# Two matmul groups of a block's preparation moved into the two-bank place of the attention scores, parts of the keys moved to GpSimd, and the first maxima taken over two banks

## The chip, the core and the metric

The kernel runs on one core of one Trainium2 chip. The metric is the device time of a whole launch in microseconds (us), the median of several runs. Engines are named as the profile names them: PE (TensorE, matmuls), PEld (its weight loads), DVE (VectorE), ACT (ScalarE), POOL (GpSimd) and SP (SyncE, which here issues nearly all DMAs).

## The reference, cut to what matters

```
# x: (1, 4096, 256); 16 heads of 16; r = 32
proj = quant4(x) @ ternary_weight(Wqkv).T + b      # one projection for Q, K and V
q = proj.reshape(B, N, h, dk).transpose(0, 2, 1, 3)
k = v = proj.reshape(B, h, N, dk)                  # a head's keys: 256 rows of proj
q, k = rotary(q), rotary(k)
att = (q @ U) @ (k @ U).T / sqrt(dk)               # i.e. q (U U^T) k^T
y = softmax(att) @ v
x = layernorm(x + quant4(y) @ ternary_weight(Wo).T)
x = layernorm(x + ffn(x))                          # 256 -> 1024 -> 1024 -> 1024 -> 256
```

`quant4` scales each row by its largest magnitude and rounds it to whole numbers from -8 to 7. `ternary_weight` gives signs, with zeros below a threshold, times a row's mean magnitude.

## The kernel before, in words

The work is cut into 8 blocks of 512 rows and 8 pairs of heads. A *unit* is one pair of heads against one block of queries, so there are 64; the first eight units are pair 0 with blocks 0 to 7. A unit has 32 *steps*. In a step s PE does three things for different units:

- `largest(s)`: two matmuls (L632), one for each head of the pair, make 128x512 scores each in a bank of PSUM from the pool `ps_1` (three banks), and two DVE reductions (L640) take their row maxima. This is a first pass that finds the largest score of each query.
- `weights(s - 40)`: 40 steps later (`LAG`), four matmuls (L678) make the scores less the maxima in a place of two banks, called `sc` (pool `ps_sc`, two such places, used in turn), and one ACT exponential of 128x1024 (L686) writes them to SBUF as `pr`.
- `values`: every second step, eight matmuls (L700) multiply two steps' `pr` with V into `av`.

So for the first 40 steps there is only the first pass (the *ramp*), and then both passes run side by side. A new unit's maxima have to go through DRAM to become rows (`largest_parts` L652 and L653, `largest_rows` L659 to L667) before its `weights` can start.

The order on all engines is written out by hand. `at(step, f)` puts a piece of work into a list, and the loop at the end calls, for each step, what is listed for it and then `largest` and `weights`. A step is thus only a place in each engine's order. An engine does its own list as soon as its data are there; GpSimd and SP can be far ahead of or behind PE's step.

Within the ramp and pair 0, the seven later blocks are also prepared, each during one unit. For block b, with `first = 32(b-1)`:

- the block of x is loaded 24 steps ahead, its row maxima are taken on DVE (`biggest`, L129, four times), and POOL makes the whole numbers (`integers`, L148 to L152);
- at first+5, `tables`: the rows' scale goes through DRAM and comes back spread over all partitions (L445, L447), and the cosines are loaded (L337);
- at first+7, `transposed`: eight PE transposes (L158) and an ACT copy (L160);
- at first+9 and first+11, `even_odd`: the projection of the even and of the odd columns, two matmuls each (L459), into one bank of `ps_1` each; ACT scales (L467), POOL multiplies by the scale and adds the bias (L468, L469) into `eo`;
- at first+12, `queries`: POOL rotates and splits them into a high and a low part (L484 to L492); SP stores them in DRAM (L497, first+23), and loads them as `qT` of the next unit (L590, at step 25 of the unit before), so that `largest` of block b can start at step 32b;
- at first+13 and first+15, `natural`: the block's V (`project`, L170), in one bank of `ps_1` each, with ACT (L603) and later POOL (L606, L607);
- at first+16, `rotate_keys` on POOL (L510 to L513), at first+29 `regroup_keys` by DMA (L521), at first+34 and first+36 `times_g`: the keys times U U^T (L529, one matmul instruction of two passes each), into one bank of `ps_1` each; ACT copies the high part (L531), DVE makes the low part (L532); SP stores them (L570) for the later pairs.

Block 0 is prepared ahead of the ramp by `set_up`, which also prepares the signs of both weight matrices. Its keys are spread over partitions by `place_keys` (L558), in places of `sc`, one group for each of the first eight steps.

After pair 0 there are seven pairs with no block to prepare, and then the feed-forward part.

Of the kernel before, what the change touches and what calls it, by code (L numbers as in the profile page):

```python
# [9 lines left out]
F32 = mybir.dt.float32  # L10
# [8 lines left out]
P = 128  # L19
# [18 lines left out]
def attn_ffn_kernel(  # L38
# [53 lines left out]
    sgn_o = const.tile([P, 2, D], BF16, name="sgn_o")  # L92
    alpha_o = const.tile([P, D], F32, name="alpha_o")
    bias_bc = const.tile([P, D], F32, name="bias_bc")
    scales = {}
# [203 lines left out]
    with ExitStack() as actx:  # L299
# [31 lines left out]
        def bank1(shape, dt):  # L331
            return ps_1.tile(shape, dt, name="ps1")
# [7 lines left out]
        def set_up():  # L340

            nc.sync.dma_start(out=x_bufs[0], in_=x_t[:, ts(0, BT), :])
            tw = [ppool.tile([P, 2, D], F32, name=f"tw{i}", tag="pr") for i in range(2)]
            wabs = ppool.tile([P, 2, 2, D], F32, name="tabs", tag="pr")
            neg = ppool.tile([P, 2, 2, D], F32, name="tneg", tag="pr")
            nc.sync.dma_start(out=tw[0], in_=wqkvT.rearrange("(k p) o -> p k o", p=P))
            set_picks()
# [12 lines left out]
            nc.sync.dma_start(out=cs_k, in_=csk)  # L360
            ps = magnitudes(tw[0], wabs[:, 0], bank1)
            biggest(None)
# [3 lines left out]
            nc.sync.dma_start(out=x_bufs[1], in_=x_t[:, ts(1, BT), :])  # L366
            nc.sync.dma_start(out=tw[1], in_=woT.rearrange("(k p) o -> p k o", p=P))
            nc.sync.dma_start(out=bias_bc, in_=bqkv.partition_broadcast(P))

            set_constants()  # L370
            for e in range(2):
                for k in range(2):
                    nc.tensor.matmul(
                        ps[:, D + e : D + e + 1],
                        lhsT=wabs[:, 0, k, e::2],
                        rhs=ones[:, :1],
                        start=(k == 0),
                        stop=(k == 1),
                    )
# [10 lines left out]
            transposed()  # L390
            signs(tw[0], neg[:, 0], ps, sgn_qkv, alpha_qkv)
            nc.vector.tensor_scalar(alpha2, ps[:, D : D + 2], 1.0 / D, None, ALU.mult)
            nc.vector.tensor_tensor(gmat, psg[:, :P], mask, ALU.mult)

            def output_weights():
                ps = magnitudes(tw[1], wabs[:, 1], bank1)
                return lambda: signs(tw[1], neg[:, 1], ps, sgn_o, alpha_o)

            return held, output_weights

# [51 lines left out]
        def even_odd(b, held, o):  # L452
# [17 lines left out]
            else:  # L470
# [3 lines left out]
                nc.scalar.activation(x, x, AF.Identity, bias=bias2_sb[:, o : o + 1])  # L474

        def two(key):
            return [rot.tile([P, 2, QB], F32, name=f"{key}{i}") for i in range(2)]
# [48 lines left out]
        def times_g(b, held, x):  # L526
# [5 lines left out]
            nc.vector.tensor_tensor(low, ps, high.bitcast(F32), ALU.subtract)  # L532

        def place_queries(held, qT):

            ps = bank1([P, QB], F32)
            for n in range(4):
                h, i = divmod(n, 2)
                nc.tensor.matmul(
                    ps,  # L540
                    lhsT=pick_q[:, h, i],
                    rhs=held["parts"][:, h, i],
                    start=(n == 0),
                    stop=(n == 3),
                )
            nc.scalar.copy(qT, ps)

        def place_keys(held, kT, g, banks={}):

            if g % 2 == 0:  # L550
                banks[0] = ps_sc.tile([P, 2, QB], F32, name="sc")
            ps = banks[0][:, g % 2]
            for k in range(2):
                x, c = divmod(2 * g + k, 8)
                for n in range(4):
                    j, i = divmod(n, 2)
                    o = 80 - 64 * j - DK * i
                    nc.tensor.matmul(  # L558
                        ps[:, ts(k, N // H)],
                        lhsT=pick_k[:, c, o : o + P],  # L560
                        rhs=held["parts"][:, 2 + x, i, ts(j, N // H)],
                        start=(n == 0),
                        stop=(n == 3),
                    )
            nc.scalar.copy(kT[:, ts(g, QB)], ps)
# [28 lines left out]

        def natural(b, held, i0):

# [13 lines left out]

            project(held, sgn_qkv, bank1, i0, evacuate)

# [4 lines left out]
        yas, yts, y4s, ys = {}, {}, {}, {}  # L617
        todo = {}

        def at(step, f):  # L620
            todo.setdefault(step, []).append(f)

        def largest(s):

            u, i = divmod(s, NKT)
            qt, ck = divmod(i, NKT // BT)
            if i == 0:
                mxs[u] = stat.tile([P, BT, 2, NKT // BT], F32, name="mx")
            ps = [ps_1.tile([P, 512], F32, name="ps1") for j in range(2)]
            for j in range(2):  # L630
# [7 lines left out]
                )  # L638
            for j in range(2):
                nc.vector.tensor_reduce(  # L640
                    mxs[u][:, qt, j, ck : ck + 1], ps[j], AX.X, ALU.max
                )
            if i == NKT - 1:
# [173 lines left out]
        with tc.manual_schedule():  # L817
# [5 lines left out]
            at(NKT * (NQB + 2 * len(chunks)), set_flag)  # L823
            first_held, output_weights = set_up()
            even_odd(0, first_held, 0)
            even_odd(0, first_held, 1)
            output_signs = output_weights()
            rotate_keys(0, first_held, nc.vector)
# [3 lines left out]
            qTs[0] = qpool.tile([P, QB], F32R, name="qT", bufs=3)  # L832
            times_g(0, first_held, 0)
            place_queries(first_held, qTs[0])
            place_keys(first_held, kTs[0], 0)
            output_signs()
            times_g(0, first_held, 1)
            for g in range(1, 8):
                at(g - 1, lambda g=g: place_keys(first_held, kTs[0], g))
            at(2, lambda: store_queries(0, first_held))  # L840
            for i in range(2):
                at(4 + i, lambda i=i: natural(0, first_held, 2 * i))
            at(6, lambda: [f() for f in first_held["rest"]])
            for b in range(1, NQB):
                first = NKT * (b - 1)
                h, biggest, measure, integers, transposed = quantize_steps(
                    x_bufs[b % 2], bank1, nc.gpsimd, ma_parts[b % 2][:, :BT]
                )
                if b > 1:
                    at(  # L850
                        first - 24,
                        lambda b=b: nc.sync.dma_start(out=x_bufs[b % 2], in_=x_t[:, ts(b, BT), :]),
                    )
                    for i in range(BT):
                        at(first - 15 + 2 * i, lambda i=i, f=biggest: f(i))
                    for i, f in enumerate(measure):
                        at(first - 7 + 2 * i, f)
                else:
                    biggest(None)
                    for f in measure:  # L860
                        f()

                def tables(b=b, h=h):
                    start_scales(b, h)
                    h["cs"] = load_tables(b)

                at(first - 1 if b > 1 else 0, integers)
                at(first + 5, tables)
                at(first + 7, transposed)
                for o in range(2):  # L870
                    at(first + 9 + 2 * o, lambda b=b, h=h, o=o: even_odd(b, h, o))
                at(first + 12, lambda b=b, h=h: queries(b, h))
                at(first + 23, lambda b=b, h=h: store_queries(b, h))
                for i in range(2):
                    at(first + 13 + 2 * i, lambda b=b, h=h, i=i: natural(b, h, 2 * i))
                at(first + 16, lambda b=b, h=h: rotate_keys(b, h, nc.gpsimd))
                at(first + 17, lambda h=h: [f() for f in h["rest"]])
                at(first + 29, lambda h=h: regroup_keys(h))
                for x in range(2):
                    at(first + 34 + 2 * x, lambda b=b, h=h, x=x: times_g(b, h, x))  # L880
                    at(first + 37, lambda b=b, h=h, x=x: store_keys(b, h, x))

# [5 lines left out]
            for u in range(NU):  # L888
# [12 lines left out]
                if u:  # L901
                    at(NKT * (u - 1) + (25 if u < NQB else 14), lambda u=u: load_queries(u))
                base = NKT * u + LAG
# [48 lines left out]
            for s in range(NKT * NU + LAG + AVLAG + 4):  # L952
                while todo.get(s):
                    todo[s].pop(0)()

# [217 lines left out]
```

## Time and profile before

| | |
|---|---|
| median of 3 runs | 3589.16 us (3588.69 to 3589.31) |
| the profiled execution | 3586.87 us |
| its span in the profile | 3585.0 us |
| PE busy | 3544.8 us (99%) |
| DVE busy | 3044.8 us (85%) |
| ACT busy | 2337.1 us (65%) |
| POOL busy | 432.2 us (12%) |
| first exponential (the ramp's end) | 91.01 us |
| last exponential | 2907.13 us |

Busy time is counted from the start of an instruction to its modelled end, so a PE that is shown 100% busy can still lose time between matmuls. The time from one `values` group to the next (a *pair of steps*) is the better ruler: in most of the kernel it is 2.70 us.

### The profile page before, as it was taken

The numbers are of one execution on the slowest core, as the hardware profiler recorded it, in microseconds if no ns is written. First come the engines' busy times: TensorE is split into PE (matmuls) and PEld (weight loads), VectorE is DVE, ScalarE is ACT, GpSimd is POOL, SyncE is SP. The second block draws the span as 40 slices with busy tenths as digits, with TensorE's granted clock in tenths as the row PEclk, the third lists the DMA queues.
The fourth block names the chain that finished last, engine by engine and source line by source line (L and its number), as shares of the span: only waits on it lengthen the run. The fifth ranks groups of instructions, "written<-read, shape, count | busy, mean of one in ns | idle before, by whom it ended". The sixth has DMA issues, their size and how long they took to land.

```text
span 3585.0 us, 61100 instructions
## 1 busy us (share of the span) xinstructions
PE 3544.8 (99%) x23824; PEld 1996.1 (56%) x23831; DVE 3044.8 (85%) x5612; ACT 2337.1 (65%) x2710; POOL 432.2 (12%) x525
## 2 busy tenths in 40 slices
PE   7999999999999999999999999999999999999998
PEld 4444455555555555555555555545555458888887
DVE  8888999999999999999999999999999945555554
ACT  2777777777777777777777777777777753333332
POOL 5766300000000000000000000000000010000000
PEclk7999999999999999999999999999999999999999
DMA  3343212111211121112111111211121130000000
GB/s 92 91 112 100 58 27 50 27 27 27 50 27 29 30 50 27 27 27 51 28 27 43 34 27 27 44 27 23 47 68 33 24 91 1 29 25 18 18 7 13
DMA packets 267634, 141.74 MB, mean 40 GB/s; under 512 B 184520, under 2 KB 243656, under 8 KB 266440
## 3 DMA queue, kind: packets, MB, share of 16 engines
q1 hardware_dynamic: 263512, 126.22, 14.3%
q0 software_dynamic: 3824, 11.54, 1.1%
q8 instruction: 189, 3.10, 0.4%
q14 instruction: 109, 0.89, 0.1%
HBM read 91.44 MB, written 42.07 MB: 37 GB/s over the span
## 4 chain that ended last, share of the span: by engine, by line
PE 93%; POOL 2%; DVE 2%; DMA 2%; ACT 0%; issue 0%; SPq 0%; POOLq 0%; ACTq 0%
PE av L700 27%; PE sc L678 25%; PE ps L632 21%; PE ps_mm L997 18%; DVE mx L640 1%; DMA qT<-q_dram 1%; DMA scale<-ma_dram 0%; PE ps L529 0%; DMA ma_dram<-ma_turned 0%; POOL eo L469 0%; POOL qk L492 0%; POOL eo L468 0%; DMA q_dram<-qk 0%; POOL rot L484 0%; POOL rot L485 0%
## 5 line engine op out<-in xcount | busy, mean ns | idle before, releaser
L640 DVE TENSOR_REDUCE mx<-ps 128x1 f32<-128x512 f32 x4096 | 2550.0, 683 | 147.4 <-PE ps L632 93.1
L686 ACT ACTIVATE pr<-sc 128x1024 f32<-128x1024 f32 x2048 | 1991.6, 1021 | 739.4 <-PE sc L678 737.2
L632 PEld LDWEIGHTS ps<-kT,qT 64*128 64x128 f32 x4096 | 567.3, 184 | 985.2 <-DVE mx L640 852.1
L700 PE MATMUL av<-pr,v_all 128*32 128x512 f32 x8192 | 1091.6, 605 | 0.7
L632 PE MATMUL ps<-kT,qT 64*128 64x512 f32 x4096 | 1064.5, 474 | 10.0 <-DMA qT<-q_dram 4.0
L678 PE MATMUL sc<-m_rows,minus 64*128 64x512 f32 x4096 | 821.6, 394 | 0.4 <-DMA m_rows<-m_dram 0.4
L678 PE MATMUL sc<-qT,kT 64*128 64x512 f32 x4096 | 816.3, 392 | 0.0
L678 PEld LDWEIGHTS sc<-m_rows,minus 64*128 64x128 f32 x4096 | 392.6, 185 | 88.0 <-ACT pr L686 36.1
L678 PEld LDWEIGHTS sc<-qT,kT 64*128 64x128 f32 x4096 | 392.9, 184 | 86.7
L700 PEld LDWEIGHTS av<-pr,v_all 128*32 128x32 f32 x8192 | 161.3, 108 | 256.6 <-issue 254.7
L1027 ACT ACTIVATE gate<-ps_mm,sc_hs 128x512 f32<-128x512 f32 x128 | 88.1, 689 | 288.7 <-PE ps_mm L997 248.6
L281 DVE CAST h<-gate 128x512 fp32r<-128x512 f32 x128 | 54.3, 425 | 223.6 <-ACT gate L1027 223.4
L653 POOL TENSOR_TENSOR m_parts<-m,m_parts 128x8 fp32r<-128x8 f32 x64 | 13.0, 203 | 1798.7 <-ACT m_parts L652 1763.5
L283 DVE TENSOR_TENSOR h<-gate,h 128x512 fp32r<-128x512 f32 x192 | 132.3, 689 | 5.1
L997 PE MATMUL ps_mm<-h,h1a 128*128 128x512 f32 x512 | 128.8, 394 | 0.0
L1019 DVE SCALAR_TENSOR_TENSOR gate<-ps_mm,sc_s,gate 128x512 f32<-128x512 f32 x64 | 48.0, 750 | 94.3 <-ACT gate L1017 74.3
L997 PE MATMUL ps_mm<-h,h2a 128*128 128x512 f32 x512 | 127.2, 390 | 0.0
L997 PE MATMUL ps_mm<-h,h1b 128*128 128x512 f32 x512 | 126.5, 389 | 0.0
L997 PE MATMUL ps_mm<-h,h2b 128*128 128x512 f32 x512 | 126.5, 389 | 0.0
L732 DVE STREAM_TRANSPOSE yt<-ya 128x64 f32<-128x64 f32 x504 | 116.8, 232 | 0.0
L997 PEld LDWEIGHTS ps_mm<-h,h1b 128*128 128x128 f32 x512 | 96.1, 188 | 20.1
L997 PEld LDWEIGHTS ps_mm<-h,h2b 128*128 128x128 f32 x512 | 96.1, 188 | 19.9
(178 smaller groups left out, 1636.8 us busy)
## 6 DMA issues: line engine op xcount, KB each, us to landing
y_raw<-yt SPq DMA_DIRECT2D x256, 64.0 KB
qT<-q_dram SPq DMA_DIRECT2D x252, 64.0 KB
y<-y_raw SPq DMA_DIRECT2D x63, 256.0 KB
kT<-k_dram SPq DMA_DIRECT2D x28, 512.0 KB
xs<-in_x SPq DMA_DIRECT2D x16, 512.0 KB
q_dram<-qk SPq DMA_DIRECT2D x32, 256.0 KB
k_dram<-qk SPq DMA_DIRECT2D x56, 128.0 KB
cs_q<-in_csq SPq DMA_DIRECT2D x8, 512.0 KB
```

What stands on the lines that cost most here:

```text
L281: eng(dst[:, k, 0, :], g)
L283: nc.vector.tensor_tensor(dst[:, k, 1, :], g, dst[:, k, 0, :].bitcast(F32), ALU.subtract)
L632: nc.tensor.matmul(ps[j], lhsT=qTs[u][rows, ts(qt, P)], rhs=kTs[u // NQB][rows, ts(ck, 512)], start=True, stop=True,)
L640: nc.vector.tensor_reduce(mxs[u][:, qt, j, ck : ck + 1], ps[j], AX.X, ALU.max)
L653: nc.gpsimd.tensor_tensor(parts[:, :, 1, :], m, parts[:, :, 0, :].bitcast(F32), ALU.subtract)
L678: nc.tensor.matmul(ps[:, j, :], lhsT=minus[rows, :] if first else kTs[u // NQB][rows, ts(kt, P)], rhs=m_rows[u % 2][rows, :] if first else ...
L686: nc.scalar.activation(pr, ps, AF.Exp)
L700: nc.tensor.matmul(avs[u][strip : strip + 32, :], lhsT=v_all[:, 2 * (2 * pair + j) + a, c * (DK + 1) : c * (DK + 1) + 32], rhs=probs[s + k ...
L732: nc.vector.transpose(yts[u][:, ts(i, 64)], yas[u][:, ts(i, 64)])
L997: nc.tensor.matmul(ps, lhsT=sb[:, ks, ts(o, P)] if split else wo[:, k, :], rhs=src[:, k, i, :], start=(k == 0 and i == 0), stop=(k == n - ...
L1019: nc.vector.scalar_tensor_tensor(g, pb, scales["s2"][:, o : o + 1], gate, ALU.mult, ALU.mult)
L1027: nc.scalar.activation(g, ps, AF.Gelu, scale=scales[sc][:, o : o + 1])
```

## The change

It has five parts.

1. From block 2 on, `both_projections` takes the place of the two `even_odd`, `all_natural` that of the two `natural`, and `both_times_g` that of the two `times_g`. Each makes all its matmuls in one go into one two-bank place of `sc`, the places that otherwise hold the scores of `weights`. ACT empties the projections and the products with one 128x1024 copy each, V with four 128x256 ones as before.
2. `key_parts` splits the keys on GpSimd (a copy and a subtraction of 128x1024), where `times_g` used ACT and DVE. The projections' scale, factor and bias are all applied on GpSimd.
3. The steps of a block's preparation change. `tables` comes 8 steps before the unit for blocks 3 and later, x is loaded 30 steps ahead, and the queries of units 4 to 7 are loaded at step 22 where it was 25. The three groups are put into a second list, `later`, so that they stand behind `values` in their step.
4. In the ramp, `largest` puts its two matmuls into one place of `sc`, and one DVE reduction takes both maxima (128x1024 to 128x2). In unit 0 it goes through the keys chunk by chunk, so that a chunk is needed every fourth step only; `place_keys` moves to every second step and into `ps_1`.
5. The output weights' signs leave `set_up`: their sums are taken in the ramp (step 20) and their signs on GpSimd, later. The second block's maxima are taken before the ramp starts, and its preparation moves by some steps.

The core of the diff:

```diff
+        def both_projections(held):
+            held["eo"] = kprep.tile([P, 2, QB], F32, name="eo", tag="kr")
+            ps = ps_sc.tile([P, 2, QB], F32, name="sc")
+            for o in range(2):
+                for k in range(2):
+                    nc.tensor.matmul(ps[:, o], lhsT=sgn_qkv[:, k, o::2], ...)
+            nc.scalar.copy(held["eo"], ps)
+            nc.gpsimd.tensor_tensor(held["eo"], held["eo"], held["scale"]..., ALU.mult)
+            for o in range(2):
+                x = held["eo"][:, o]
+                nc.gpsimd.tensor_scalar(
+                    x, x, alpha2[:, o : o + 1], bias2_sb[:, o : o + 1], ALU.mult, ALU.add
+                )
...
+        def both_times_g(held):
+            ps = ps_sc.tile([P, 2, QB], F32, name="sc")
+            for x in range(2):
+                nc.tensor.matmul(ps[:, x], lhsT=gmat, rhs=held["keys"][:, x], start=True, stop=True)
+            held["kg"] = kprep.tile([P, 2, QB], F32, name="kg", tag="kr")
+            nc.scalar.copy(held["kg"], ps)
+
+        def key_parts(held):
+            high, low = (held["parts"][:, 2:4, i] for i in range(2))
+            nc.gpsimd.tensor_copy(high, held["kg"])
+            nc.gpsimd.tensor_tensor(low, held["kg"], high.bitcast(F32), ALU.subtract)
...
-        def place_keys(held, kT, g, banks={}):
-            if g % 2 == 0:
-                banks[0] = ps_sc.tile([P, 2, QB], F32, name="sc")
-            ps = banks[0][:, g % 2]
+        def place_keys(held, kT, g):
+            ps = bank1([P, QB], F32)
...
+        def all_natural(b, held):
+            both = ps_sc.tile([P, 2, QB], F32, name="sc")
+            for i in range(2):
+                natural(b, held, 2 * i, lambda shape, dt, i=i: both[:, i])
...
-            qt, ck = divmod(i, NKT // BT)
+            qt, ck = divmod(i, NKT // BT) if u else divmod(i, BT)[::-1]
...
-            ps = [ps_1.tile([P, 512], F32, name="ps1") for j in range(2)]
+            both = ps_sc.tile([P, 2, QB], F32, name="sc") if s < LAG else None
+            ps = [ps_1.tile(...) if both is None else both[:, j] for j in range(2)]
...
+            if both is not None:
+                nc.vector.tensor_reduce(mxs[u][:, qt, :, ck], both, AX.X, ALU.max)
...
-                at(first - 1 if b > 1 else 0, integers)
-                at(first + 5, tables)
-                at(first + 7, transposed)
...
+                    at(first + 2 if b == 2 else first - 4, integers)
...
+                t = (9, 11, 13, 14, 17, 18, 19, 24, 28, 31, 34)
+                if b > 2:
+                    late = {3: 6, 4: 4}.get(b, 2)
+                    t = [-8] + [n + late for n in (1, 3, 4, 5, 6, 7, 18, 23, 27, 29)]
+                    t[10] = 34 if b == 3 else t[10]
+                at(first + t[0], tables)
+                at(first + t[1], transposed)
+                behind(first + t[2], lambda h=h: both_projections(h))
+                at(first + t[3], lambda b=b, h=h: queries(b, h))
+                behind(first + t[4], lambda b=b, h=h: all_natural(b, h))
+                at(first + t[5], lambda b=b, h=h: rotate_keys(b, h, nc.gpsimd))
+                at(first + t[6], lambda h=h: [f() for f in h["rest"]])
+                at(first + t[7], lambda b=b, h=h: store_queries(b, h))
+                at(first + t[8], lambda h=h: regroup_keys(h))
+                behind(first + t[9], lambda h=h: both_times_g(h))
+                at(first + t[10], lambda h=h: key_parts(h))
...
-                    at(NKT * (u - 1) + (25 if u < NQB else 14), lambda u=u: load_queries(u))
+                    at(NKT * (u - 1) + (25 if u < 4 else 22 if u < NQB else 14), ...)
...
-                while todo.get(s):
-                    todo[s].pop(0)()
+                for work in (todo, later):
+                    while work.get(s):
+                        work[s].pop(0)()
```

## The prediction, made before the changed kernel ran

> **What bounds the kernel now.** I read the page's busy rows first, then its chain of waits, then PE in order of time, then the other engines in the stretches where PE loses time.
>
> ```profile
> PE 3544.8 (99%) x23824; PEld 1996.1 (56%) x23831; DVE 3044.8 (85%) x5612; ACT 2337.1 (65%) x2710; POOL 432.2 (12%) x525
> PE 93%; POOL 2%; DVE 2%; DMA 2%; ACT 0%; issue 0%; SPq 0%; POOLq 0%; ACTq 0%
> ...
> 30.00:60.00 30.00, 26.58 (x113) 14.98 (x112) 26.34 (x46) 9.68 (x19) 24.47 (x22) 0.84 0.14 45
> 60.00:90.00 30.00, 28.30 (x53) 12.55 (x55) 25.85 (x49) 2.25 (x5) 20.10 (x20) 0.50 0.31 85
> 420.00:450.00 30.00, 30.00 (x228) 15.35 (x220) 28.44 (x52) 22.16 (x25) 4.49 (x5) 1.00 0.21 49
> ```
>
> PE bounds it (first two lines). The table by stretches (length; busy PE, PEld, DVE, ACT, POOL; clock) says where it is not so: in the ramp DVE is the full engine and PE has half its clock (0.50). The change touches the ramp and pair 0 alone. Exponentials start at 91.0 us and unit 7's at 441.5, so at most some 440 us are in play, and only what they hold above need can go.
>
> PE in order of time gives the ruler. From one `values` group (L700) to the next is 2.70 us when nothing is inserted. With something inserted the surplus is its price:
>
> ```profile
> 138.56 1.07 PE L700 MATMUL av<-pr,v_all 128*32 128x512 f32 x8
> 139.55 0.50 PE L632 MATMUL ps<-kT,qT 64*128 64x512 f32 x2
> ...
> 141.43 0.38 PE L459 MATMUL ps<-qT,sgn_qkv 128*128 128x512 bf16 x1
> 141.95 1.06 PE L700 MATMUL av<-pr,v_all 128*32 128x512 f32 x8
> ```
>
> Here 141.95 - 138.56 = 3.39, so half a projection costs 0.69 us. Read so, blocks 3 to 7 pay: transposes 0.71 to 0.90, projections 0.69 twice, V 0.9 and 0.7, products 1.14 and 1.31 to 1.60; about 6.4 us a block, 33.2 for the five with 1.3 of block 5's that belongs to the next point. Pairs with nothing inserted lose 5.7 us more, waiting for the queries:
>
> ```profile
> PE ps L632 <- DMA qT<-q_dram: 4.0, 3, 1.7
> POOL eo L468 <- DMA scale<-ma_dram: 60.3, 5, 16.5
> ...
> 282.00:284.00 2.00, 2.00 (x11) 0.66 (x12) 0.69 (x1) 0.00 (x0) 1.92 (x3) 0.70 0.45 72
> 284.00:286.00 2.00, 2.00 (x7) 0.83 (x4) 1.29 (x2) 0.83 (x1) 1.82 (x3) 0.50 0.06 17
> ```
>
> The second line is their cause: POOL stands idle 10 to 16 us a block for the scale, and the queries come late. The last two: after the stall of 1.74 us that ends at 281.75, the clock is halved for about 3.4 us.
>
> **The change part by part.**
>
> *The ramp.* First, the start. DVE now takes its first maximum at 30.98, having done the output weights' signs (25.50 to 27.9). Without them PE is the limit: keys' first group to 27.3, a second group (1.14, by L558's spacing), half of V (0.55) and the first scores (0.5) bring DVE's start to 29.5. Following PE and DVE step by step with those durations, DVE ends step 12 at about 48.5; before, that was at 50.6: -2.1. Second, the maxima. Before, two of 512 cost 2 x 0.60 when back to back (2.39 for four). No row has a 128x1024 reduction from PSUM; the nearest, L129 from SBUF, is 1.21, less 0.07 of overlap 1.14. The two ends are 1.13 (one fixed part saved) and 1.22 (none). But with two places only, PE's answer counts at half clock: weight load 0.3, matmuls 0.8, signals 0.1, so (1.14 + 1.2)/2 = 1.17 a step. That leaves 27 x 0.02 = -0.5. Third, block 2's transposes leave the ramp (-1.0, paid below), and DVE's two idle stretches for L531 (1.71 and 1.62) shrink by about half a microsecond each, as two places hold more work (-1.0). Sum -4.6; ends -2.5 (1.22, and the idle time stays) and -8 (1.13, and none of it stays).
>
> *The first steps of both passes, and block 2.* From the first scores (89.76) to the first `values` (98.69) is 8.9 us with both projections and half of V in it; without these but with the transposes I get 8.1, -0.8. They go into pairs: block 2 pays its three groups there (1.7 + 1.6 + 2.75, next part) where it paid 0.69 + 1.14 + 2.08: +2.1. Sum +1.3.
>
> *The three groups.* Matmul time is unchanged: 4 x 0.23 for the projections, 8 x 0.115 for V, 2 x 1.02 for the products (L529). Around each there is a gap, read from above: 0.69 paid for 0.46 of matmuls, so 0.23. Fewer groups save gaps, but the place of scores has a wait of its own:
>
> ```profile
> 106.85 1.94 ACT L686 ACTIVATE pr<-sc 128x1024 f32<-128x1024 f32 x2 [0.76 <-PE sc L678]
> 108.50 0.51 PE L632 MATMUL ps<-kT,qT 64*128 64x512 f32 x2
> 108.84 0.39 PE L678 MATMUL sc<-m_rows,minus 64*128 64x512 f32 x2
> 109.07 0.39 PE L678 MATMUL sc<-qT,kT 64*128 64x512 f32 x2
> 109.30 0.40 PE L678 MATMUL sc<-m_rows,minus 64*128 64x512 f32 x2
> ```
>
> A group stands at 108.50, behind `values`. One score step (108.84) follows into the other place, and the second (109.30) needs the group's place again, 0.80 us after the group's end. ACT answers 0.26 later (its start of 106.85 against PE's 106.59) and copies 1.02: the second step waits about 0.55. So a group costs 0.92 + 0.23 + 0.55 = 1.7, V 1.6, products 2.75 (the gap hidden partly). With transposes at 0.75 a block pays 6.8; five pay 34.0 against 33.2: +0.8. Behind the waiting matmul stands all of PE. The ends are no wait (-0.55 for each of 15) and twice that.
>
> Here a rule bears on it. The Trainium skill, page "TensorE: Matmul & The Clock Gate", section "Part 2: What happens when you issue a matmul", says that PE pulls weight loads ahead of running matmuls, so that inserted matmuls would cost their streaming alone: 0.46 where the row shows 0.69. By the rule the 15 groups would be 15 x 0.23 = 3.5 us cheaper. I take the row.
>
> *The queries' waits.* With the scale fetched 8 steps before the unit, POOL's chain for block 3 on starts with the projection's copy. From that: 0.9 + 1.3 to the copy, 2.4 + 2 x 1.58 scale and bias (L484's size, L469), 11.1 queries, 3.3 store, 2.7 issue and 6.3 to 7.4 load, 33 us. Block 3 has 23 steps (35 us), block 4 has 25 (38), later ones 27: the 5.7 go. `key_parts` adds 0.61 x 2 + 2.4 = 3.6 us to POOL's 36 of some 50 a block; it ends about 5 us or more before the next `eo` needs its buffer. L532's 1.4 us leave DVE, which is not the bound there. Two pointers in one scalar instruction: no row; between 0.53 (L149, constants) and 3.1 (twice L469); I take 1.58.
>
> *Block 2.* It has no early scale, and its projection stands at step 45, so 19 steps (32 us) to its queries' first use, 18 to its products. Shifted by the ramp, the copy ends at 96, POOL's queries at 112.6, rotation at 119.9. On SP:
>
> ```profile
> 111.41 3.81 SPq L497 DMA_DIRECT2D q_dram<-qk  x4
> 117.24 2.69 SPq L590 DMA_DIRECT2D qT<-q_dram  x4
> 120.83 3.03 SPq L521 DMA_DIRECT2D keys<-rot  x4
> ```
>
> In the new order the next block's scale and cosines stand between the first two of these and wait for a landing; the keys are issued to 124.2 and land near 125.5. PE wants them at 121.5: +4 (0 to 7). Then the clock: by the section "Part 1: The HAM clock gate" of that page a whole idle window of some 3.4 us halves it, and 4 us may or may not hold one; the trace halved it after 1.74 us. By the rule nothing or 1.7, by the row 1.7 (3.4 us at half speed). I take +1.7.
>
> Output weights: PE's 2.1 us at half clock and ACT's work fall into the ramp, where DVE has a place in stock; GpSimd's signs (some 4.4) have idle time from unit 7 on. Zero; without the stock, at most 2.
>
> Sum: -4.6 + 1.3 + 0.8 - 5.7 + 4 + 1.7 = -2.5. The profiled execution took 3586.87 (span 3585.0), 2.3 under the median of 3589.16; the difference is applied to the median: 3586.7.
>
> **The rivals.** 0.2% is 7.2 us, about what a measurement of this kernel tells from no change. Forecast: within it, 0.5.
> *The groups don't wait*, and the ramp's reductions come at 1.13: -2.5 - 18 x 0.55 - 1 = -13.4, 3576; or block 2 is not late, -8.2, 3581. For it: ACT is 35% idle. Against: the 0.80 above. 0.35.
> *A group holds back two score steps*: ACT, behind by 1.02, is late for the next step as well, and each of 18 groups costs 0.6 us more: +10.8 - 2.5 = +8.3, 3597. It decides from a group price of 0.55 above mine. For it: DVE and ACT both hang on PE's rhythm. Against: ACT has 0.76 free in each pair. 0.15.
>
> The range reaches from 3576 to 3596.
>
> **What would show it.** The ramp's first exponential near 86; pairs with a group at 4.3 to 4.4 us (projections, V) and 5.45 (products), with PE waiting for ACT's copy; no wait for queries after block 3; a wait for the keys of block 2, with half clock behind it. I am wrong if pairs with a group are under 4.0, or if block 2's products start on time.

## The result, and the profile after

The changed kernel takes 3606.02 us (median of 5 runs, 3604.52 to 3607.22), against 3588.69 (3587.68 to 3589.31) for the kernel before: a ratio of 1.0051, with an interval of 1.0040 to 1.0062. It is slower by about 17 us, where 3586.7 had been forecast, in a range that ended at 3596. The profiled execution took 3605.85, with a span of 3604.1 (before 3585.0), so the spans differ by 19.1 us.

Lines have new numbers after the change: `largest` is L709 (matmuls), L720 and L717 (reductions of 512 and of two banks); `weights` L758, its exponential L766; `values` L780; the products with U U^T L587; V L171. On SP, the scale is L468 (to DRAM) and L470 (back), the cosines L338, the queries L652, the keys' regrouping L570.

First the page's rows of busy time and of the chain of waits, then the stretches that were shown of before (length; busy PE, PEld, DVE, ACT, POOL; clock; DMA share; GB/s):

```profile
PE 3531.9 (98%) x23831; PEld 1988.4 (55%) x23831; DVE 3035.9 (84%) x5554; ACT 2335.6 (65%) x2700; POOL 446.7 (12%) x536
PE 94%; POOL 2%; DVE 2%; DMA 1%; ACT 0%; issue 0%; SPq 0%; POOLq 0%; ACTq 0%; DVEq 0%
...
30.00:60.00 30.00, 23.73 (x120) 13.33 (x119) 26.62 (x26) 9.85 (x20) 24.19 (x18) 0.86 0.40 126
60.00:90.00 30.00, 22.08 (x73) 10.27 (x75) 27.23 (x35) 5.55 (x8) 17.91 (x23) 0.63 0.28 81
420.00:450.00 30.00, 30.00 (x228) 15.22 (x220) 28.83 (x54) 22.09 (x24) 0.00 (x0) 1.00 0.14 32
```

PE is busy for 13 us *less* than before, and the span is 19 us longer. PE has more idle time, then, and the chain's row, still 94% PE, does not show where. PE's waits from 80 to 420 us do (engine, what, line, what it waits for: total us, times, longest):

```profile
PE sc L587 <- DMA keys<-rot: 18.1, 4, 5.9
PE sc L171 <- ACT v_all L665: 5.6, 6, 0.9
PE ps L709 <- DMA qT<-q_dram: 2.0, 1, 2.0
...
PE sc L758 <- ACT eo L512: 1.6, 6, 0.3
```

The products wait for the block's keys to be regrouped by DMA, four times, 18.1 us in all. In PE's order of time, block 4:

```profile
233.25 1.06 PE L780 MATMUL av<-pr,v_all 128*32 128x512 f32 x8
238.79 3.20 PE L587 MATMUL sc<-keys,gmat 128*128 128x512 f32 x4 [4.48 <-DMA keys<-rot]
241.92 0.80 PE L709 MATMUL ps<-kT,qT 64*128 64x512 f32 x2
...
244.04 1.06 PE L780 MATMUL av<-pr,v_all 128*32 128x512 f32 x8
```

Between the two `values` groups lie 10.79 us instead of 2.70. PE stands for 4.48 us (in brackets). The products' modelled length is 3.20 and not the 1.98 of the undisturbed block 7, and the two score matmuls behind them take 0.80 us, not 0.50. Why, the stretches around them show (same columns):

```profile
236.00:238.00 2.00, 0.00 (x0) 0.00 (x0) 0.00 (x0) 0.00 (x0) 0.00 (x0) 1.00 0.95 188
238.00:240.00 2.00, 1.21 (x2) 0.59 (x3) 0.00 (x0) 0.00 (x0) 0.00 (x0) 0.84 0.69 124
240.00:242.00 2.00, 2.00 (x5) 0.42 (x3) 0.00 (x0) 0.00 (x0) 0.00 (x0) 0.50 0.01 3
```

From 236 to 238 no engine works at all, while the DMA engines are 95% busy; from 240 on the clock is halved. So a late DMA is paid twice, once as idle time and once as half clock.

**The ledger.** The surplus of a pair of steps over 2.70 us, summed over the pairs of the first eight units (computed from the traces):

| us | before | after | forecast for a group |
|---|---|---|---|
| first exponential | 91.01 | 83.77 | |
| first exponential to first `values` | 7.68 | 6.87 | |
| projections | 6.96 | 8.35 (6 x 1.39) | 1.7 |
| V | 8.66 | 13.57 (6 x 2.26) | 1.6 |
| transposes | 3.92 | 3.55 | 0.75 |
| products | 17.60 | 41.14 (6 x 6.86; the undisturbed one 2.32) | 2.75 |
| pairs with nothing inserted | 8.33 | 5.70 | |

The surpluses rise by 26.8, the start gains 8.0, together +18.8 of the 19.1 us between the spans. The products of blocks 2 to 7 cost 10.05, 4.78, 8.09, 8.53, 7.37 and 2.32 us; for block 3, 3.51 more lie in the pair before, where PE waits 1.99 us for the queries and then runs at half clock. What blocks 3 to 6 pay beyond 2.32 is 23.0 us: that is the whole loss and more.

**Why the keys are late.** SP in order of time, around block 4's keys:

```profile
217.00 3.14 SPq L652 DMA_DIRECT2D qT<-q_dram  x4
225.42 0.57 SPq L468 DMA_DIRECT2D ma_dram<-ma_turned  x1
227.87 0.34 SPq L470 DMA_DIRECT2D scale<-ma_dram  x1
228.25 0.62 SPq L338 DMA_DIRECT2D cs_q<-in_csq  x1
228.91 0.59 SPq L640 DMA_DIRECT2D kT<-k_dram  x1
229.61 2.48 SPq L570 DMA_DIRECT2D keys<-rot  x4
```

On POOL the rotation of block 4's keys has long ended (start, length):

```profile
221.30 1.29 POOL L562 TENSOR_TENSOR rot<-rot,rot 128x512 f32<-128x512 f32 x1
```

The keys were ready at 222.6 and issued from 229.6 to 232.1. In between stands `tables` of the *next* block, block 5, moved by the change to 8 steps before its unit: SP has nothing issued between 220.1 and 225.42, since it stands at L468 and waits for DVE to turn the maxima (at that step of DVE's order); then L470 waits for L468's data to land. And the keys, issued to 232.1, reach PE only at 238.79, 6.7 us later, since the scale, the cosines and `kT` are under way beside them.

### The profile page after: what moved, and what is told of

Its sections match the earlier page's. It is cut to its first block, busy times and chain, and to the rows that moved or that the text cites. A ratio compares the mean times of both kernels' runs of the same rounds, so it can differ in the third digit from the quotient of the medians.

```text
span 3604.1 us, 60963 instructions
## 1 busy us (share of the span) xinstructions
PE 3531.9 (98%) x23831; PEld 1988.4 (55%) x23831; DVE 3035.9 (84%) x5554; ACT 2335.6 (65%) x2700; POOL 446.7 (12%) x536
## 4 chain that ended last, share of the span: by engine, by line
PE 94%; POOL 2%; DVE 2%; DMA 1%; ACT 0%; issue 0%; SPq 0%; POOLq 0%; ACTq 0%; DVEq 0%
PE av L780 27%; PE sc L758 26%; PE ps L709 21%; PE ps_mm L1114 18%; DVE mx L717 1%; DMA keys<-rot 1%; PE sc L587 1%; DVE mx L720 0%; DMA qT<-q_dram 0%; POOL qk L541 0%; POOL rot L560 0%; POOL rot L559 0%; PE ps_mm L1156 0%; PE ps_mm L171 0%; ACT eo L512 0%
## 5 line engine op out<-in xcount | busy, mean ns | idle before, releaser
L720 DVE TENSOR_REDUCE mx<-ps 128x1 f32<-128x512 f32 x4016 | 2501.7, 684 | 184.5 <-PE ps L709 133.3
L766 ACT ACTIVATE pr<-sc 128x1024 f32<-128x1024 f32 x2048 | 1990.7, 1021 | 719.1 <-PE sc L758 718.3
L780 PE MATMUL av<-pr,v_all 128*32 128x512 f32 x8192 | 1092.0, 605 | 0.0
L709 PEld LDWEIGHTS ps<-kT,qT 64*128 64x128 f32 x4016 | 545.5, 183 | 947.2 <-DVE mx L720 827.5
L709 PE MATMUL ps<-kT,qT 64*128 64x512 f32 x4016 | 1015.9, 471 | 3.0 <-DMA qT<-q_dram 2.0
L758 PE MATMUL sc<-m_rows,minus 64*128 64x512 f32 x4096 | 817.9, 394 | 3.2 <-ACT eo L512 1.6
L758 PE MATMUL sc<-qT,kT 64*128 64x512 f32 x4096 | 813.3, 392 | 0.0
L758 PEld LDWEIGHTS sc<-m_rows,minus 64*128 64x128 f32 x4096 | 389.5, 185 | 88.6 <-ACT pr L766 35.0
L758 PEld LDWEIGHTS sc<-qT,kT 64*128 64x128 f32 x4096 | 388.0, 185 | 87.7
L780 PEld LDWEIGHTS av<-pr,v_all 128*32 128x32 f32 x8192 | 161.4, 108 | 255.8 <-issue 255.0
```

Source lines behind the costliest of these rows:

```text
L709: nc.tensor.matmul(ps[j], lhsT=qTs[u][rows, ts(qt, P)], rhs=kTs[u // NQB][rows, ts(ck, 512)], start=True, stop=True,)
L720: nc.vector.tensor_reduce(mxs[u][:, qt, j, ck : ck + 1], ps[j], AX.X, ALU.max)
L758: nc.tensor.matmul(ps[:, j, :], lhsT=minus[rows, :] if first else kTs[u // NQB][rows, ts(kt, P)], rhs=m_rows[u % 2][rows, :] if first else ...
L766: nc.scalar.activation(pr, ps, AF.Exp)
L780: nc.tensor.matmul(avs[u][strip : strip + 32, :], lhsT=v_all[:, 2 * (2 * pair + j) + a, c * (DK + 1) : c * (DK + 1) + 32], rhs=probs[s + k ...
```

## The experiments

Two theories for the loss of 23 us in blocks 3 to 6. *SP's order*: the next block's scale and cosines hold the keys back. Rivals: *GpSimd*, slowed by the new work, ends the rotation late; *landing*: the regrouping takes 6 us whatever stands ahead of it. For V: the second half's matmuls wait for ACT's copies out of the first half, as both are in one place of `sc`.

The kernel before took 3589.46 us beside the first four, 3588.12 beside the next four, 3587.47 beside the last two. Ratios are against these, with their 95% intervals.

**1. The next block's tables behind the keys** (one number: `tables` at 2 steps before the unit, not 8, for blocks 3 and later).

```diff
-                    t = [-8] + [n + late for n in (1, 3, 4, 5, 6, 7, 18, 23, 27, 29)]
+                    t = [-2] + [n + late for n in (1, 3, 4, 5, 6, 7, 18, 23, 27, 29)]
```

> One edit to the changed kernel: for blocks 3 to 7 the scale and the cosines are fetched at first-2 and not at first-8, so that on SP they stand behind the keys' regrouping of the block before. No other engine's work changes. Theory SP (the keys are issued late because SP holds, ahead of them, a DMA that waits for DVE's step, and another that waits for its landing): the products of blocks 3 to 6 start on time, a pair with products costs 2.3 to 2.6 us there in place of 4.8, 8.1, 8.5 and 7.4, block 3's wait for queries goes, block 2 keeps most of its wait; together -20 to -25 us, 3581 to 3586. Rival GpSimd (the keys are late because GpSimd has 3.4 us a block more to do): no change of that size, 3603 to 3606, and the wait for keys stays in blocks 4 to 6. Rival landing (a keys' DMA takes 6 us whatever is before it): the waits shrink by the earlier issue only where it is early enough, that is as theory SP, but block 2 keeps all of its 5.9 us.

Measured: 3577.4 us (3575.91 to 3577.91), ratio 0.9967 (0.9954 to 0.9979): 28.6 us less than the change, from one number, and more than the 20 to 25 expected. SP in order of time, then PE, for the same block 4 (both of this kernel):

```profile
203.87 3.06 SPq L652 DMA_DIRECT2D qT<-q_dram  x4
...
208.22 3.06 SPq L570 DMA_DIRECT2D keys<-rot  x4
...
220.98 0.62 SPq L468 DMA_DIRECT2D ma_dram<-ma_turned  x1
```

```profile
220.08 1.06 PE L780 MATMUL av<-pr,v_all 128*32 128x512 f32 x8
221.07 1.98 PE L587 MATMUL sc<-keys,gmat 128*128 128x512 f32 x4
```

The keys leave 10 us before PE wants them, L587 has no bracket, and it takes 1.98. The products cost 2.42 on the mean, the sum of surpluses is 42.5 instead of 72.3, no queries are waited for, and the clock stays up. What remains of the wait is block 2's:

```profile
PE sc L587 <- DMA keys<-rot: 0.5, 1, 0.5
```

There the keys are issued to 118.3 and used at 120.26, so they land within 2 us when nothing else of size is under way. The GpSimd theory falls, as POOL's work was not touched; the landing theory falls, as block 2's wait went from 5.9 to 0.5 us. But theory SP, too, had left block 2 most of its wait, so the hold is not the whole cause; experiment 5 has the rest.

**2. V's eight matmuls ahead of its four copies.**

```diff
-                natural(b, held, 2 * i, lambda shape, dt, i=i: both[:, i])
+                natural(b, held, 2 * i, lambda shape, dt, i=i: both[:, i], after)
+            for f in after:
+                f()
```

> One edit to the changed kernel: in a block's V all eight matmuls are issued before the four ACT copies, so that the second half does not wait for the first half's copies. The 0.93 us before the second half goes and a pair with V costs 1.4 in place of 2.26. If waits only add up, 6 blocks gain 5 to 5.6 us: 3600.5. If, as I think, PE then only arrives sooner at the wait for keys (blocks 2, 4, 5, 6) or queries (block 3), whose time is set by the projection ahead of V, only block 7 gains: -1 to -2, 3604 to 3605.

Measured: 3603.52 (3602.36 to 3605.43), ratio 1.0041 (1.0027 to 1.0056). V first as it stands in the changed kernel, then here, both in PE's order of time:

```profile
201.76 0.61 PE L171 MATMUL sc<-sgn_qkv,qT 128*128 128x256 bf16 x4
...
203.30 0.60 PE L171 MATMUL sc<-sgn_qkv,qT 128*128 128x256 bf16 x4 [0.93 <-ACT v_all L665]
```

```profile
200.78 1.05 PE L171 MATMUL sc<-sgn_qkv,qT 128*128 128x256 bf16 x8
...
203.49 0.50 PE L766 MATMUL sc<-m_rows,minus 64*128 64x512 f32 x2 [0.76 <-ACT v_all L665]
```

The wait in the middle is gone, and most of it comes back at the score step that needs the same place (here `weights` is L766): V costs 1.90 instead of 2.26, not the 1.4 expected. The place of `sc` is held until ACT has emptied all of it, in whatever order. And the time went down by no more than 2.5 us, as the products still cost 6.80 on the mean.

**3. The ramp's and block 1's part alone** (blocks 2 and later prepared by the operations and at the steps of before, but for block 2's whole numbers, which stay at the changed kernel's first+2).

```diff
-                behind(first + t[2], lambda h=h: both_projections(h))
+                for o in range(2):
+                    at(first + 9 + 2 * o, lambda b=b, h=h, o=o: even_odd(b, h, o))
...
-                behind(first + t[9], lambda h=h: both_times_g(h))
-                at(first + t[10], lambda h=h: key_parts(h))
+                for x in range(2):
+                    at(first + 34 + 2 * x, lambda b=b, h=h, x=x: times_g(b, h, x))
```

> The ramp's part of the change alone: set-up, ramp and block 1 as in the changed kernel, blocks 2 to 7 with the operations and steps of the kernel before. The first exponential comes near 84 as in the changed kernel (91.0 before). Theory: block 2's chain through GpSimd and DRAM is no faster than before, so PE waits some 4 us for its queries at step 64 and the ramp's 7 us shrink to 3: 3585 to 3586. Rival (the ramp's gain is kept in full): 3581 to 3582.

Measured: 3583.07 (12 runs, 3579.85 to 3586.65), ratio 0.9982 (0.9974 to 0.9991): about -6.4 us, between the two expectations. The first exponential starts at 86.14, not at 83.8, since block 2's transposes are back at first+7 and its whole numbers, three steps later than in the kernel before, come too late for them (experiment 9 sets them back and starts at 83.80). Its PE waits have:

```profile
PE ps L159 <- POOL qint L153: 2.8, 1, 2.8
```

**4. Three edits at once**: 1 and 2, and block 2's products and keys' parts 4 steps later.

```diff
-                t = (9, 11, 13, 14, 17, 18, 19, 24, 28, 31, 34)
+                t = (9, 11, 13, 14, 17, 18, 19, 24, 28, 35, 38)
```

> The changed kernel with the edits of the first two kernels and block 2's products and the split of its keys 4 steps later (steps 67 and 70 in place of 63 and 66). Theory: the waits for keys and their half clock go in all blocks, so V's 0.9 a block now counts: about 9 to 12 us under the first of these kernels, 3571 to 3575, and faster than the kernel before by 0.35 to 0.5%. Rival (a wait for block 2's queries at step 64 takes the place of the one for its keys): 3576 to 3579.

Measured: 3574.68 (3574.02 to 3574.88), ratio 0.9958 (0.9942 to 0.9975). No wait for keys or queries is left; products 2.36 on the mean. It is 2.7 us below experiment 1, and at the upper end of what was expected.

**5. The scale stays early, only the cosines go behind the keys.** In the changed kernel the scale's two DMAs wait, and the cosines (512 KB) fill the DMA engines. Which of the two is the cost?

```diff
-                at(first + t[0], tables)
+                at(first - 8, lambda b=b, h=h: start_scales(b, h))
+                at(first - 2, cosines)
```

> The changed kernel with one half of the first experiment's edit: for blocks 3 to 7 the scale stays at first-8, ahead of the keys of the block before on SP, and only the cosines (512 KB) are fetched at first-2, behind them. Theory traffic (what makes the keys late is chiefly that they land behind the cosines and scale: 6 us from issue in the changed kernel, about 2 in the first experiment): keys are issued some 0.6 us earlier but land in 2 to 3 us, so the waits in blocks 4 to 6 nearly go and 3577 to 3582 comes out. Theory hold (SP, stopped ahead of the keys until DVE reaches its step, is enough): the waits and the half clock stay in blocks 4 to 6 at 3 us or more each, 3593 to 3601.

Measured: 3588.48 (3585.59 to 3589.89), ratio 0.9999 (0.9991 to 1.0008), between the theories, so the blocks have to be told apart. Products of blocks 2 to 7: 8.74, 2.33, 4.64, 2.73, 2.81, 2.32. In blocks 4 to 6 they lose 3.2 us beyond 3 x 2.32, where the changed kernel loses 17.0: there 13.8 us go with the cosines. The hold is still there. For block 5, POOL ends the rotation at 266.5, SP issues the keys from 273.97 on, and PE does not wait for them, as they land within 2 us (POOL, SP and PE of this kernel):

```profile
265.19 1.28 POOL L562 TENSOR_TENSOR rot<-rot,rot 128x512 f32<-128x512 f32 x1
273.97 2.48 SPq L570 DMA_DIRECT2D keys<-rot  x4
278.17 1.95 PE L587 MATMUL sc<-keys,gmat 128*128 128x512 f32 x4 [0.37 <-ACT pr L766]
```

So held keys cost little if they land quickly. The other half, keys that land slowly but are not held, was not run for these blocks. An estimate from the changed kernel's block 4: ready at 222.6, with 2.5 us of issue and 6.7 of landing, they would be there at 231.8, ahead of PE's arrival at 234.3. There it takes both. Block 2, whose keys are not held (all ready at 116.4, issued from 116.00 to 118.6), is nearly as bad as in the changed kernel. SP, PE and the stretch in which PE waits, of this kernel:

```profile
116.00 2.58 SPq L570 DMA_DIRECT2D keys<-rot  x4
118.62 0.60 SPq L338 DMA_DIRECT2D cs_q<-in_csq  x1
119.40 0.49 SPq L944 DMA_DIRECT2D xs<-in_x  x1
```

```profile
123.68 3.75 PE L587 MATMUL sc<-keys,gmat 128*128 128x512 f32 x4 [4.01 <-DMA keys<-rot]
```

```profile
120.00:122.00 2.00, 0.00 (x0) 0.00 (x0) 0.00 (x0) 0.00 (x0) 1.92 (x4) 1.00 0.87 269
```

The cosines and a block of x (512 KB each) are issued *behind* the keys here, and yet the keys, issued by 118.6, arrive at 123.68, 5.1 us later, while 269 GB/s are moving. In experiment 1 SP waited at this place for L468's data to land, which put the cosines at 121.5 and x at 122.2, and kept the DMA engines free for the keys:

```profile
120.00:122.00 2.00, 1.74 (x4) 0.67 (x4) 0.05 (x1) 0.00 (x0) 1.88 (x3) 1.00 0.06 10
```

So here a place ahead in SP's order protected the keys only when what follows was issued late enough.

**6. The keys' parts back on ACT and DVE** (experiment 4 without `key_parts`: ACT copies the high part, DVE subtracts it from the place of scores).

```diff
-            held["kg"] = kprep.tile([P, 2, QB], F32, name="kg", tag="kr")
-            nc.scalar.copy(held["kg"], ps)
+            high, low = (held["parts"][:, 2:4, i] for i in range(2))
+            nc.scalar.copy(high, ps)
+            nc.vector.tensor_tensor(low, ps, high.bitcast(F32), ALU.subtract)
```

> The kernel of the fourth experiment (scale behind keys, V's matmuls first, block 2's products later) with the split of the keys back on ACT and DVE, each in one instruction over both banks, in place of GpSimd. If DVE's time counts in these stretches, each of 6 blocks pays part of the 1.2 us of subtraction: 3576 to 3579 against 3574.7. If GpSimd's part is worth nothing: 3574 to 3575.5.

Measured: 3583.98 (3583.04 to 3586.16), ratio 0.9988 (0.9980 to 0.9997): 9.3 us more than experiment 4, more than expected. Its PE waits and one of the places:

```profile
PE sc L767 <- DVE qk L592: 9.1, 6, 1.8
...
228.65 0.50 PE L767 MATMUL sc<-m_rows,minus 64*128 64x512 f32 x2 [1.47 <-DVE qk L592]
```

In experiment 4 the same score step waits 0.3 us six times for ACT's copy; here it waits 9.1 in all, and the products cost 3.71 on the mean instead of 2.36, which is 8.1 of the 9.3 us. ACT's copy has to be followed by DVE's subtraction before the place is free. The prediction gave the move to GpSimd nothing ("DVE, which is not the bound there"); as the products now stand in a place of scores, it is worth 9 us in this order, because the place is free after one copy.

**7. V in single banks again, two steps apart** (with `tables` and block 2's steps as in 4).

```diff
-                behind(first + t[4], lambda b=b, h=h: all_natural(b, h))
+                for i in range(2):
+                    at(first + t[4] + 2 * i, lambda b=b, h=h, i=i: natural(b, h, 2 * i))
...
-                at(first + t[6], lambda h=h: [f() for f in h["rest"]])
+                at(first + t[6] + 1, lambda h=h: [f() for f in h["rest"]])
```

> The kernel of the fourth experiment with V back in single banks, half a block two steps after the other, as in the kernel before. A pair with half of V cost 0.9 and 0.7 us there, the group costs 1.89: -0.3 for each of 6 blocks, 3572.5 to 3573.5. If the two-bank group is worth having (rival), it is slower by 1 us or more.

Measured: 3570.42 (3570.08 to 3570.7), ratio 0.9949 (0.9933 to 0.9966). More than expected: V costs 0.55 + 0.70 a block instead of 1.89 (from block 3 on its first half stands in the projections' pair, and 0.55 is what that pair pays beyond 1.39), and the sum of surpluses falls to 36.4. V was better off in two single banks.

**8. The kernel before with the scale early, and nothing else** (x and its maxima 6 steps earlier, `tables` 2 steps before the unit for blocks 3 and later).

```diff
-                at(first + 5, tables)
+                at(first - 2 if b > 2 else first + 5, tables)
```

> The kernel before, with x loaded and its maxima taken 6 steps earlier and the scale and cosines of blocks 3 to 7 fetched at first-2 in place of first+5; nothing else of the change. The prediction's step on the queries says that GpSimd's wait for the scale is the cause of PE's waits for queries (5.7 us in all): they go, 3583 to 3584. Rival (they are made by the keys' loads of the next pair, which come at the same time): 3587 to 3589.

Measured: 3579.72 (3577.96 to 3581.07), ratio 0.9978 (0.9968 to 0.9987): -8.4 us, more than expected. PE waits for no queries any more, and GpSimd's five waits for the scale have become one, block 2's:

```profile
POOL eo L468 <- DMA scale<-ma_dram: 15.5, 1, 15.5
```

Pairs with nothing inserted lose 1.07 instead of 8.33, products 14.92 instead of 17.60.

**9. The ramp's part and the early scale, without any group** (3 and 8 together; block 2's whole numbers one step before its unit).

```diff
-                    at(first + 2 if b == 2 else first - 4, integers)
+                    at(first - 1, integers)
...
-                at(first + t[0], tables)
+                at(first - 2 if b > 2 else first + 5, tables)
```

> Set-up, ramp and block 1 of the changed kernel, blocks 2 to 7 with single-bank operations as in the kernel before, and the eighth experiment's early scale (behind the keys); no group and no split of keys on GpSimd. If the groups are worth nothing, the two gains add up: the ramp's 7 us and the eighth experiment's 8.4, 3573 to 3575 (3588.1 - 14), or somewhat less if block 2 is held up. If the groups on the place of scores are worth more than their waits, it stays above the seventh experiment (3570.4) by 3 us or more.

Measured: 3573.85 (3572.52 to 3574.66), ratio 0.9963 (0.9949 to 0.9977). The two gains add up, as the first theory had it. The first exponential is at 83.80, as with the change. Unit 0's exponentials, beside block 2's preparation, take 54.40 (51.98 in 7), with a wait of 1.7 for the next unit's queries and 0.8 for block 2's whole numbers. Units 1 to 5, beside which blocks 3 to 7 are prepared in both kernels, take 247.4 us here, with projections and products in single banks, and 245.4 in experiment 7, with both as groups. By the ruler, projections cost 1.39 a block either way, products 2.49 here and 2.33 as a group. So the groups themselves are worth next to nothing, about 0.2 us a block; V, in single banks in both, costs 1.60 here and 1.25 in 7, where it stands elsewhere.

**10. Experiment 7 again, beside 9.**

> The seventh experiment's kernel once more, on the same chip as the ninth: 3569 to 3572 by every theory; it is there so that the two can be compared.

Measured: 3570.03 (3569.44 to 3570.28), ratio 0.9953 (0.9936 to 0.9970). It is the best version, 17.4 us under the kernel before and 36 under the change; experiment 9 is 3.8 us longer, and 4.9 between the two profiled executions, of which 2.9 lie in unit 0 (51.48 us here), with block 2's preparation, and 2.0 in units 1 to 5.

## Why the prediction was wrong

**The step that failed: "The queries' waits".** It followed the moved scale along GpSimd's chain alone, found that chain ready in time ("the 5.7 go"), and stopped; what the move does to the keys of blocks 3 to 6 it put at nothing, without a reason. That GpSimd is no longer late is right. But the same two DMAs and the cosines were moved past others in SP's order too: with `tables` of block b+1 8 steps before its unit, they stand ahead of block b's keys. Block 4's keys were issued 7.0 us after they were ready, and then took 6.7 us to land beside the cosines and `kT`. Either alone would have cost little (3.2 us in blocks 4 to 6 for the first, by experiment 5; nothing for the second, by the estimate there). The prediction did see that order, and even said that they "wait for a landing", but under "Block 2", as if it were that block's trouble. It holds for every block that has a successor with an early scale. The pairs of blocks 3 to 6 pay 23.0 us for it; experiment 1 takes it all away with one number, and experiment 8 shows that the early scale was worth 8.4 us in the kernel before, when the keys are not held.

Most signs that the prediction named did come: groups' pairs above 4.0 us (4.09 and 4.96), no wait for queries after block 3, block 2's wait for its keys with half clock behind it. None of them looks at the keys of the later blocks.

**Block 2's keys.** Forecast: "the keys are issued to 124.2 and land near 125.5", PE wanting them at 121.5. They came at 125.65, but by another route: GpSimd was 3.4 us earlier than worked out (116.5, not 119.9), the keys were issued by 119.60, and they took 6 us to land where 1.3 was assumed. (Of the 3.4 us, 1.6 are the bias step: with two pointers it took 0.77 us each time, and not 1.58.) PE arrived at 119.79, so it waited 5.86, not 4. With half clock (forecast +1.7, and it came) this is 7.7 us against 5.7. The terms mis-sized are the issue, too late by 4.6 us, and the landing, too short by 4.7: that they nearly cancel is luck. Without the cosines and x beside them the keys landed in 2 us (experiment 1).

**The ramp.** Forecast -4.6, measured -7.2 at the first exponential. The reduction was sized right; eleven of them, one behind the other, on DVE:

```profile
39.78 12.55 DVE L717 TENSOR_REDUCE mx<-sc 128x2 f32<-128x1024 f32 x11 [0.94 <-PE sc L709]
```

That is 1.14 us each, as estimated. What was too careful is the limit of 1.17 from PE at half clock and the idle time that was left to remain; the granted clock from 60 to 90 us was 0.63 and not 0.50. How much each of these gave was not measured. The first steps of both passes gained 0.8, as forecast.

**The groups.** Projections were priced at 1.7 and cost 1.39, products at 2.75 and cost 2.32 undisturbed: the second score step waits 0.28 us for ACT (L758 for `eo`) and not 0.55. V was priced at 1.6 and cost 2.26. Its step failed in treating V as one group; `all_natural` empties the first half before the second half's matmuls, and these wait 0.93 us for ACT although they go into the other bank. In the sum +4.0 for V against -1.9 and -2.6 for the others: no great error, but one with a cause that can be fixed (experiment 7).

**The sum, mended.** -2.5 forecast, +23.0 for blocks 3 to 6, +2.0 for block 2, +4.0 for V, -1.9 for projections, -2.6 for products, -2.6 for the ramp: +19.4. The spans differ by 19.1.

**The rivals.** "The groups don't wait" is near the truth for projections and products, and did not decide. "A group holds back two score steps" gave the right sign for a wrong reason: behind the score step that waits for the group's place no further one waits, and the groups are under their price. By the rule on weight loads pulled ahead a group would have no gap around its matmuls: for the projections 1.39, less 0.92 of matmuls and 0.28 of wait, leaves 0.19, near the 0.23 of the row; for the products 2.32, less 2.04 and 0.28, leaves nothing. The case that came, the keys of every block held back in SP's order and landing beside the cosines, was in no rival, though its pieces (SP's order before and after, and 4 us for one block) stood in the text.

## What to carry to other kernels

When a DMA is moved earlier, list what stands behind it on the issuing engine up to its old place, in every round of the loop, and ask of each when it is wanted: a DMA that has to wait holds them all, and a large one shares the engines with those issued next to it on either side. A group in a place that another stage needs costs as long as the place is held, so empty it with one instruction of one engine, and do the rest from SBUF. And when a change has several parts, look for the one number that could turn its sign: here a step of -8 or -2 was 28.6 us of 3600.

## What the runs showed of the hardware

- The regrouping of four times 128 KB was there within 2 us of its last issue alone or with no more than the scale's 256 KB beside it (experiment 1, block 2; experiment 5, blocks 5 and 6), and 4.1 to 6.7 us after it with cosines, x or `kT`, 512 KB each, under way (the change, blocks 2 and 4 to 6; experiment 5, blocks 2 and 4), whether these were issued before or after it. The Trainium skill, page "DMA: Bandwidth & Descriptors", section "Issuing engines are not separate DMA queues", says that DMAs run on the same 16 engines and interleave, whichever engine started them; the delays fit that, for DMAs that all have one issuer, SP.
- The clock changes on a fixed grid of 3.41 us: in each of the traces here, every stretch at one clock between two changes is a whole number of such meshes. In the changed kernel the five stalls bring half clock from 123.31 to 130.14, 181.34 to 188.17, 239.37 to 242.78, 290.57 to 297.39 and 348.59 to 352.00 us: one or two meshes of 3.41 each, with 15, 15, 14 and 15 meshes between. What counts is PE's idle time within one mesh, not the length of a stall. From 95 to 480 us, in the traces of all kernels here, half clock followed every mesh at full clock in which PE was idle for 1.67 us or more (13 times) and none with 1.47 or less; of the two between, 1.60 was followed by it and 1.64 was not. So a stall of 1.99 us halved the clock in the change (idle 1.60 us of a mesh, by two waits), and one of 2.21 in experiment 5, which falls into two meshes with 0.97 and 1.24 idle, did not (first the change, then experiment 5, each mesh as one stretch):

```profile
177.93:181.34 3.41, 1.81 (x11) 0.96 (x11) 2.44 (x5) 2.25 (x4) 2.01 (x3) 1.00 0.51 124
181.34:184.75 3.41, 2.37 (x9) 0.48 (x9) 0.69 (x1) 0.00 (x0) 0.00 (x0) 0.50 0.33 70
```

```profile
225.36:228.77 3.41, 2.44 (x20) 1.09 (x16) 2.48 (x4) 1.94 (x2) 1.52 (x2) 1.00 0.88 186
228.77:232.19 3.42, 2.17 (x6) 0.84 (x8) 0.00 (x0) 0.08 (x1) 0.00 (x0) 1.00 0.66 114
232.19:235.60 3.41, 3.15 (x24) 1.37 (x24) 2.80 (x5) 2.94 (x4) 2.33 (x2) 1.00 0.62 189
```

  The Trainium skill, page "TensorE: Matmul & The Clock Gate", section "Part 1: The HAM clock gate", asks for at least one idle window of about 3.4 us, free-running. The grid fits that window; that it has to be idle throughout does not fit, as 1.67 us were enough. In the ramp idle time alone does not tell: in the kernel before, at 47 us, 0.66 was enough.
- A second matmul group into the other bank of a two-bank place waited for ACT's reads of the first bank (0.93 us, six times). Whether the chip or only the program's bookkeeping by places asks for this was not tried.
